# Local-attention layers on one core: finer pieces of scores and values' sums, weights one layer ahead, the norm on POOL, and a new order of issue

## The chip, the cores and the metric

The kernel runs on one core of one Trainium2 chip. The metric is device time in microseconds of one execution. Three runs of the kernel before gave 5607.32, 5605.51 and 5598.71 us; the median is 5605.51 us. One more execution was taken with the hardware profiler, and every duration below comes from it.

## The reference

The input is 16 sequences of 256 rows and 128 columns, float32. Four blocks follow one another, each as `x = x + layernorm(block(layernorm(x)))`. The first three (attention with low-rank weights, a routed expert layer, plain attention) are not touched by the change. The fourth is a stack of six layers, and it takes more than half of the time:

```
def attn_layer(x, Wqkv, qs, ksc, Wo):
    q, k, v = split(x @ Wqkv)            # 16 heads of 64
    q = l2norm(q) * qs;  k = l2norm(k) * ksc
    q = q*cos*scale + rotate_half(q)*sin*scale
    k = k*cos/scale + rotate_half(k)*sin/scale
    return local_attention(q, k, v) @ Wo # windows of 32: a row sees its own window and the one before
def ffn_layer(x, g, bln, W1, b1, W2, b2):
    a, gate = split(layernorm(x)*g + bln) @ W1 + b1
    return a * gelu(gate) @ W2 + b2
for i in range(6):
    x = attn_layer(shift_tokens(x), ...) + x
    x = ffn_layer(shift_tokens(x), ...) + x
```

`shift_tokens` takes the right half of the columns from the row before. `l2norm` divides each head's row by `maximum(norm, 1e-12)`.

## The kernel before

**One unit of work is one sequence in one layer.** There are 6 x 16 = 96 of them, numbered n; layer n // 16, sequence n % 16. Each unit is cut into some hundred named operations (`xT`, `pq0`, `sk1`, ...), each of which is a handful of instructions of one engine. The string `PERIOD` (line 770) lists all operation names once, each with a lag: at step s, `pq0:2` works on unit s - 2. `block4` (line 779) runs the steps one after another and, in each step, goes through the list from left to right. So several units are in flight, each in another part of its work.

**The list is the order of issue.** The class `InOrder` (line 35) ties each instruction of an engine to the one issued before it on the same engine, DMA issues on SyncE (SP) among them. An engine never takes a later instruction first: an operation that waits holds everything that stands behind it on its engine.

**What the names mean**, with t = 0 or 1 for the two halves of 128 rows, and a, b for halves of the heads:

- TensorE: `xT` transposes x; `pq`, `pk`, `pv` project (4 matmuls of 512 columns each); `tq`, `tk` transpose q and k; `sc` are the scores (128 small matmuls a half); `pe` transposes the exponentials; `pc` are the values' sums (128 small matmuls a half); `wo`, `gh`, `w2` are the output and feed-forward products; `gx` transposes the normed rows.
- VectorE: `a` multiplies the projection with the rotary tables; `r` sums the squares; `ms` and `mx` read the scores from PSUM, mask them and take their maximum; `sm` sums the exponentials; `y1` and `y0` add to x; `bn` takes mean and variance for the feed-forward norm; `xn` is that norm; `st` is the gate.
- ScalarE: `s` squares, `l` does Ln and Exp for the inverse norm, `x` is the exponential, `c..`, `ce`, `cc`, `cv` and `xc` copy PSUM to SBUF, `gg` is gelu (between two table loads).
- POOL: `h` and `m` finish the rotation and the scaling, `sb` subtracts the maximum, `n` normalises, `rs` raises the variance to the power -0.5.
- SP, all by DMA: `dv0` (16 DMAs) and `dv1` (14) spread v, one DMA for each window and half of the heads, into the windowed tile `vw`, each value once for its own window and once as the next window's past; `xs` (3 DMAs) moves x shifted by a row into the tile `xs` for `bn`; `W...` load weights.
- Units of layer 0 also pass `i1`, `i2`, `i3` (keep a copy, then norm), units of layer 5 `f1` to `f4` (norm, add, store).

**Buffers.** PSUM is two pools: `ps_p` with 3 buffers of 128x1024 (projections, `sc`, `pc`, two thirds of `gh`) and `ps_1` with 2 buffers of 128x512 (everything else). `xs`, `kT`, `vw` exist twice and are used by even and odd units.

**Weights** have one buffer each for `wo`, `w1`, `w2`, and five for the three parts of Wqkv. `Wqk` loads two parts and `Wv` the third, 512 KB each, at a layer's first unit; the v part needs the buffer of a q part that the layer before still uses.

Near the operations of the prediction the list of before reads, on each engine in its order:

```
SP:   dv0:3  dv1:3  xs:4  tb:0  Wqk:0
DVE:  ... ak1:3 bn:5 rk1:3 aq0:2 xn:5 rq0:2 ak0:2 ms0:3 ...  sm1:3 y1:4 aq1:2 rq1:2
ACT:  sk1:3 ce0b:4 xc:1 lq1:3 sq0:2 ck0a:3 ce1a:4 cv0:3 ...
POOL: hq1:3 mq1:3 rs:5 hk1:3 mk1:3 hq0:2 hk0:2 sb0:3 mq0:2 sb1:3 mk0:2 n0:3 n1:3
```

Of the kernel before, what the change touches and what calls it, by code (L numbers as in the profile page):

```python
# [1 line left out]

# [9 lines left out]
FP = mybir.dt.float32  # L12
# [52 lines left out]
class Net:  # L65
# [690 lines left out]
    def table(self, ins):  # L756
# [14 lines left out]
        xT:1 pq0:2 Wv:1 sk1:3 hq1:3 ce0b:4 pe1a:4 xc:1 lq1:3 ak1:3 mq1:3 sq0:2 tk0a:3 bn:5 i1:0 ck0a:3 pc0:4  # L771
        rk1:3 aq0:2 ce1a:4 rs:5 i2:0 tk0b:3 cv0:3 xn:5 i3:0 hk1:3 lk1:3 ck0b:3 pk0:2 cc0:4 tq1a:3 pe1b:4 dv0:3
        mk1:3 sk0:2 cq1a:3 rq0:2 sc0:3 ak0:2 tq1b:3 ms0:3 dv1:3 ce1b:4 tk1a:3 ck1a:3 pc1:4 hq0:2 cq1b:3 tk1b:3
        ck1b:3 mx0:3 hk0:2 sb0:3 w2:7 W2:6 y0:7 f1:7 cc1:4 gx:5 sc1:3 xg:5 lq0:2 rk0:2 mq0:2 x0:3 ms1:3 mx1:3
        f2:7 gh:5 W1:4 sb1:3 lk0:2 gg:5 pv1:2 pq1:2 sm0:3 f3:7 x1:3 wo:4 Wo:3 mk0:2 sq1:2 st:5 n0:3 sm1:3 f4:7
        cv1:2 y1:4 aq1:2 tq0a:2 pk1:2 n1:3 tq0b:2 rq1:2 cq0a:2 xs:4 cq0b:2 tb:0 pe0a:3 pv0:2 ce0a:3 pe0b:3 Wqk:0
# [14 lines left out]
    def layer_ops(self, ctx):  # L791
# [13 lines left out]
        rope = self.load(cp, "rope", ins["rope"].rearrange("k (t p) d -> p k t d", p=128), [128, 4, 2, LH])  # L805
# [5 lines left out]
        nc.gpsimd.memset(tiny[:, 1:2], EPS)  # L811
# [111 lines left out]
        def moments(n, src):
            st = self.small.tile([128, 2, 6], FP, name="bn_st")
            mv = put(n, "mv", self.small.tile([128, 2, 2], FP, name="bn_mv"))
            for t in range(2):
                nc.vector.bn_stats(st[:, t, :], src[:, t, :])
            for t in range(2):
                nc.vector.bn_aggr(mv[:, t, :], st[:, t : t + 1, :])
            ve = put(n, "ve", self.small.tile([128, 2], FP, name="bn_ve"))  # L930
            nc.vector.tensor_tensor(ve, mv[:, :, 1], tiny[:, 1:2].to_broadcast([128, 2]), ALU.add)

        def inverse(n):
            rstd = put(n, "rstd", self.small.tile([128, 2], FP, name="bn_rstd"))
            nc.gpsimd.tensor_tensor(rstd, take(n, "ve"), self.half.to_broadcast([128, 2]), ALU.pow)

        def norm(n, dst, src):
            mv, rstd = take(n, "mv"), take(n, "rstd")
            for t in range(2):
                nc.vector.scalar_tensor_tensor(  # L940
                    dst[:, t, :],
                    src[:, t, :],
                    mv[:, t, 0:1],
                    rstd[:, t : t + 1].to_broadcast([128, D]),
                    ALU.subtract,
                    ALU.mult,
                )
# [94 lines left out]
        @by("r", heads_of)  # L1042
        def _(n, k, t):
            r = put(n, ("r", k, t), pool.tile([128, NH], FP, name="r", bufs=6))
            sq = take(n, ("sq", k, t)).rearrange("p (h d) -> p h d", d=LH)
            nc.vector.tensor_reduce(r, sq, AX.X, ALU.add)
            nc.vector.tensor_tensor(r, r, tiny[:, 0:1].to_broadcast([128, NH]), ALU.max)

        @by("l", heads_of)
        def _(n, k, t):  # L1050
            r = get(n, ("r", k, t))
            nc.scalar.activation(r, r, AF.Ln)
# [38 lines left out]
        def _(n, t):  # L1091
            v = put(n, ("v", t), pool.tile([128, 2, 8, LH], FP, name="v"))
# [17 lines left out]
        @by("sc", tiles_of)  # L1110
        def _(n, t):
            s = put(n, ("s", t), ps_p.tile([128, 2, 8, 64], FP, name="sc", tag="p"))
            qT, kT = take(n, ("qT", t)), kTs[n % 2]
            for c in range(8):
# [66 lines left out]
        @by("pc", tiles_of)  # L1181
        def _(n, t):
            p = put(n, ("pc", t), ps_p.tile([128, 2, 4, 128], FP, name="pc", tag="p"))
            eT, vw = (take(n, ("eT", t, 0)), take(n, ("eT", t, 4))), vws[n % 2]
            for d in range(4):
                for q in range(4):
                    for odd in range(2):
                        c = 2 * d + odd
                        for j in range(2):
                            r, o = slice(64 * j, 64 * j + 64), 64 * (j ^ odd)  # L1190
                            nc.tensor.matmul(
                                p[o : o + 64, odd, d, 32 * q : 32 * q + 32],
                                lhsT=vw[r, 4 * t + q, c, :],
                                rhs=eT[c // 4][r, c % 4, 32 * q : 32 * q + 32],
                                start=True,
                                stop=True,
                            )
# [7 lines left out]
        def _(n):  # L1205
            po = put(n, "po", ps_1.tile([128, 2, D], FP, name="po", tag="w"))
            for t in range(2):
                cT = take(n, ("cT", t))
                for c in range(8):
                    nc.tensor.matmul(po[:, t, :], lhsT=cT[:, c, :], rhs=w["o"][:, c, :], start=c == 0, stop=c == 7)  # L1210
# [38 lines left out]
        def _(n):  # L1249
# [153 lines left out]
```

## Time and profile before

| | us |
|---|---|
| median of the three runs | 5605.51 |
| profiled execution, its own time | 5580.84 |
| its span, first to last instruction | 5579.1 |
| first three blocks, to the first transpose of the six layers | 2157.5 |
| six layers, from there to the end | 3421.6 |
| layers 1 to 4: from the first unit's `xT` of layer 1 (2661.8) to that of layer 5 (4901.3), 64 steps | 2239.5, or 35.0 a step |
| TensorE busy in 2638 to 3197, about layer 1 | 521.2 of 559.0 |
| VectorE, ScalarE, POOL busy there | 471.5, 358.5, 414.0 |

A busy time says how long an engine had an instruction in work, and nothing on whether the end waits for it. The granted clock of TensorE is 0.98 of full speed in that stretch. In the rows below, "idle before" is the time in which the engine had nothing in work just before such an instruction, and the name behind the arrow is what ended it; SPq is the DMA-issuing sequencer of SyncE. Nearly all lines of the fourth block are shown as L45, which is the helper in `InOrder`, so tiles' names tell the operations apart: `vw<-v` is `dv`, `xs<-x` is the shift, `bn_st` is `bn`, `x<-po` is `y0` or `y1`.

### The profile page before, as it was taken

How to read it: one execution, taken by the hardware profiler on the slowest of the kernel's cores; microseconds unless marked ns; L12 is line 12 of the kernel's file. 1: busy time of each engine (PE TensorE's matmuls, PEld its weight loads, DVE VectorE, ACT ScalarE, POOL GpSimd, SP SyncE). 2: the span in 40 equal slices, each digit the busy share in tenths (PEclk: the TensorE clock that was granted, in tenths of full speed). 3: DMA queues.
4: the chain of work that ended last, by engine and by line, in shares of the span. 5: the costliest groups of instructions: out<-in, count | busy, mean ns of one | idle time of the engine just before them, and what ended most of it. 6: DMA issues, size and time to landing. Idle time of an engine off the chain costs nothing.

```text
span 5579.1 us, 171669 instructions
## 1 busy us (share of the span) xinstructions
PE 4647.6 (83%) x74492; PEld 3449.9 (62%) x74492; DVE 4023.8 (72%) x6623; ACT 2761.0 (49%) x4751; POOL 2835.4 (51%) x2042
## 2 busy tenths in 40 slices
PE   7888754444489996999899989998999899999997
PEld 5555543333356664667677767776777667667776
DVE  3443228988743335889788878887888788878996
ACT  1222212333322224766566666666666666666664
POOL 1000012223210005777677767777777777767774
PEclk9999766767788888999999999999999999999998
DMA  1000000000000001322222222222222222222322
GB/s 28 1 1 1 1 0 11 1 0 1 1 3 1 1 1 44 73 65 68 71 71 64 64 71 68 66 65 73 68 69 60 75 66 66 64 72 70 73 68 59
DMA packets 222003, 240.87 MB, mean 43 GB/s; under 512 B 107747, under 2 KB 124598, under 8 KB 221110
## 3 DMA queue, kind: packets, MB, share of 16 engines
q1 hardware_dynamic: 221254, 229.90, 17.2%
q8 instruction: 590, 9.67, 0.8%
q14 instruction: 159, 1.30, 0.1%
HBM read 24.19 MB, written 4.19 MB: 5 GB/s over the span
## 4 chain that ended last, share of the span: by engine, by line
PE 66%; DVE 17%; issue 6%; ACT 4%; POOL 3%; SPq 2%; DMA 2%; ACTq 0%; POOLq 0%; DVEq 0%
PE pp L45 15%; PE po L45 7%; PE pc L45 7%; PE s L201 6%; PE pt L45 6%; PE sc L45 5%; PE ph L45 4%; PE pe L45 2%; PE s L213 2%; SPq L45 2%; DVE w L714 2%; PE pc L294 2%; DMA xs<-x 2%; DVE a L45 1%; DVE nm L257 1%
## 5 line engine op out<-in xcount | busy, mean ns | idle before, releaser
L45 POOL TENSOR_TENSOR a<-a 128x512 f32<-128x512 f32 x768 | 968.4, 1282 | 391.5 <-DVE a L45 390.2
L45 PE MATMUL pp<-part,xT 128*128 128x512 f32 x2304 | 1087.9, 602 | 3.0 <-DVE a L45 2.2
L45 DVE TENSOR_TENSOR a<-pp,tab 128x2048 f32<-128x2048 f32 x384 | 876.7, 2283 | 118.1 <-ACT sq L45 108.3
L45 POOL TENSOR_TENSOR am<-a,r 128x1024 f32<-128x1024 f32 x384 | 731.4, 1905 | 278.6 <-issue 244.9
L126 POOL TENSOR_TENSOR bn_rstd<-bn_ve,half 128x2 f32<-128x2 f32 x128 | 92.5, 724 | 1361.6 <-DVE bn_mv L122 1248.2
L45 PEld LDWEIGHTS pp<-part,xT 128*128 128x128 f32 x2304 | 415.8, 194 | 344.8 <-issue 319.2
L45 PE MATMUL pc<-eT,vw 64*64 64x32 f32 x24576 | 467.0, 222 | 91.3 <-issue 89.6
L45 PEld LDWEIGHTS pc<-eT,vw 64*64 64x64 f32 x24576 | 433.1, 136 | 137.0 <-issue 130.2
L45 PE MATMUL pt<-ident,am 128*128 128x128 f32 x3072 | 474.6, 283 | 23.2 <-POOL am L45 9.1
L45 DVE TENSOR_REDUCE r<-sq 128x16 f32<-128x1024 f32 x384 | 463.9, 1208 | 0.0
L45 PEld LDWEIGHTS pt<-ident,am 128*128 128x128 f32 x3072 | 357.0, 144 | 145.8 <-issue 109.4
L45 POOL TENSOR_TENSOR e<-e,mx 128x1024 f32<-128x1024 f32 x192 | 365.2, 1902 | 133.6 <-DVE mx L45 130.4
L45 ACT COPY kT<-pt 128x512 f32<-128x512 f32 x384 | 223.0, 581 | 417.5 <-PE pt L45 417.3
L45 ACT ACTIVATE sq<-pp 128x1024 f32<-128x1024 f32 x384 | 395.1, 1029 | 44.1 <-PE pp L45 43.9
L730 PE MATMUL pw<-ident,w 128*128 128x128 f32 x512 | 114.9, 416 | 353.7 <-ACT w L715 353.7
L45 PEld LDWEIGHTS po<-wo,cT 128*128 128x128 f32 x3072 | 358.1, 192 | 45.1 <-issue 44.5
L45 POOL TENSOR_TENSOR e<-e,sm 128x1024 f32<-128x1024 f32 x192 | 362.4, 1905 | 9.1 <-ACT sq L45 4.5
L45 ACT COPY qT<-pt 128x512 f32<-128x512 f32 x384 | 225.9, 590 | 272.1 <-PE pt L45 272.1
L45 PE MATMUL po<-wo,cT 128*128 128x128 f32 x3072 | 358.5, 275 | 0.0
L45 PE MATMUL sc<-kT,qT 64*32 64x64 f32 x24576 | 324.0, 230 | 38.3 <-issue 25.6
L257 DVE TENSOR_REDUCE nm<-s 128x2 f32<-128x512 f32 x256 | 159.1, 685 | 263.3 <-PE s L201 263.3
L45 PEld LDWEIGHTS sc<-kT,qT 64*32 64x32 f32 x24576 | 280.0, 107 | 87.8 <-issue 52.5
(221 smaller groups left out, 9167.4 us busy)
## 6 DMA issues: line engine op xcount, KB each, us to landing
vw<-v SPq DMA_DIRECT2D x2880, 64.0 KB
part<-in_L_ffn_Wqkv SPq DMA_DIRECT2D x18, 512.0 KB
xs<-x SPq DMA_DIRECT2D x96, 64.0 KB
xs<-x SPq DMA_DIRECT2D x96, 63.5 KB
wo<-in_Wo SPq DMA_DIRECT2D x6, 512.0 KB
x<-in_L_attn_hidden_states SPq DMA_DIRECT2D x8, 256.0 KB
kept<-x SPq DMA_DIRECT2D x16, 128.0 KB
xend<-kept SPq DMA_DIRECT2D x16, 128.0 KB
```

What stands on the lines that cost most here:

```text
L45: ins = trace(*args, **kw)
L126: nc.gpsimd.tensor_tensor(rstd, ve, self.half.to_broadcast([128, n]), ALU.pow)
L201: nc.tensor.matmul(s[:, i, o : o + 128], lhsT=lhs[r, g, lcols], rhs=rhs[r, g, rcols.start + o : rcols.start + o + 128], start=not masked, ...
L213: nc.tensor.matmul(s[:, :, diag], lhsT=self.ident_bf, rhs=mask[:, 0:n, :], start=True, stop=False)
L257: nc.vector.tensor_reduce(nm[:, 1, gs[0] : gs[1] + 1, 32 * j + NMROW], s, AX.X, ALU.max, negate=True)
L294: nc.tensor.matmul(pc[32 * j : 32 * j + 32, i, cols], lhsT=va[:, t, 4 * (g + i) + j, :], rhs=e[j][:, g + i, :], start=t == 0, stop=t == 1,)
L714: nc.vector.tensor_tensor(w, w, hh.unsqueeze(1).to_broadcast([128, RH, NE]), ALU.mult)
L730: nc.tensor.matmul(pw[:, c, :], lhsT=w[:, h, bass.ts(c, 128)], rhs=self.ident, is_transpose=True, start=h == 0, stop=h == RH - 1,)
```

## The change

The diff does six things.

1. `sc` and `pc` of each half become four operations each (`sc00` to `sc13`, `pc00` to `pc13`), 32 matmuls an operation; the number and the shape of the matmuls stay. The PSUM tile is allocated by the first of the four and released after the last.
2. Weights of the next layer are loaded in 18 pieces (12 of Wqkv, 4 of Wo, 2 of W1), one DMA a step and two in a layer's last four steps, by the new operation `W` at the end of the list. Wqkv has six buffers, Wo and W1 two. All of layer 0 is loaded at step 0. The rotary table is loaded from HBM into the table's tile for each layer and scaled there.
3. The norm (`xn`, `i3`, `f3`) goes from VectorE to POOL, and the addition of epsilon goes from VectorE (end of `bn`) to POOL (start of `rs`).
4. The maximum with 1e-24 at the end of `r` on VectorE becomes a Relu with bias -1e-24 and a bias of 1e-24 in Ln, on ScalarE.
5. `sq` and `v` share one set of three buffers (before, two each); `qT` has three (before, four).
6. `PERIOD` is written anew, with other lags and another order on every engine.

```diff
     PERIOD = """
-        xT:1 pq0:2 Wv:1 sk1:3 hq1:3 ce0b:4 pe1a:4 xc:1 lq1:3 ak1:3 mq1:3 sq0:2 tk0a:3 bn:5 i1:0 ck0a:3 pc0:4
-        rk1:3 aq0:2 ce1a:4 rs:5 i2:0 tk0b:3 cv0:3 xn:5 i3:0 hk1:3 lk1:3 ck0b:3 pk0:2 cc0:4 tq1a:3 pe1b:4 dv0:3
-        mk1:3 sk0:2 cq1a:3 rq0:2 sc0:3 ak0:2 tq1b:3 ms0:3 dv1:3 ce1b:4 tk1a:3 ck1a:3 pc1:4 hq0:2 cq1b:3 tk1b:3
-        ck1b:3 mx0:3 hk0:2 sb0:3 w2:7 W2:6 y0:7 f1:7 cc1:4 gx:5 sc1:3 xg:5 lq0:2 rk0:2 mq0:2 x0:3 ms1:3 mx1:3
-        f2:7 gh:5 W1:4 sb1:3 lk0:2 gg:5 pv1:2 pq1:2 sm0:3 f3:7 x1:3 wo:4 Wo:3 mk0:2 sq1:2 st:5 n0:3 sm1:3 f4:7
-        cv1:2 y1:4 aq1:2 tq0a:2 pk1:2 n1:3 tq0b:2 rq1:2 cq0a:2 xs:4 cq0b:2 tb:0 pe0a:3 pv0:2 ce0a:3 pe0b:3 Wqk:0
+        xT:1 pv1:3 cc1:5 lk1:3 x1:4 hq1:3 tk0a:3 pq0:2 mq1:3 xc:1 tk0b:3 dv0:3 f2:8 hk1:3 sm1:4 n1:4 ck0a:3
+        mk1:3 cv1:3 pk0:2 ck0b:3 sq0:2 f3:8 sc00:3 rq0:2 pe0a:4 sk0:2 sc01:3 tq1a:3 aq0:2 ce0a:4 dv1:3 f4:8
+        sc02:3 cq1a:3 wo:5 rk0:2 lq0:2 y1:5 tq1b:3 sc03:3 xs:5 ak0:2 tk1a:3 cq1b:3 bn:5 i1:0 ms0:3 pc00:4
+        ck1a:3 pe0b:4 hq0:2 mq0:2 pc01:4 tk1b:3 mx0:3 pq1:2 ce0b:4 rs:5 i2:0 tq0a:2 ck1b:3 pc02:4 sq1:2
+        tq0b:2 cq0a:2 cq0b:2 xn:5 i3:0 hk0:2 pc03:4 rq1:2 pv0:2 aq1:2 lk0:2 cc0:4 pe1a:4 sb0:3 sc10:3 ce1a:4
+        gx:5 xg:5 mk0:2 sc11:3 x0:3 pe1b:4 sc12:3 gh:5 ce1b:4 sm0:3 cv0:2 pc10:4 sc13:3 w2:7 W2:6 ms1:3 n0:3
+        pc11:4 mx1:3 pk1:2 gg:5 pc12:4 st:5 sb1:3 lq1:2 sk1:2 rk1:2 y0:7 f1:7 ak1:2 pc13:4 W:0
     """
...
+            def parts(k, j):
+                c = bass.ts(j, 256)
+                src = ins["L1_ffn_Wqkv"][i][:, k * inner : (k + 1) * inner]
+                load("qkv"[k], j, c, [inner], src[:, c], name="part", bufs=6)
...
+            for _ in range(2 if b >= B - 4 else 1):
+                if b > 0 and w["next"]:
+                    w["next"].pop(0)()
...
-            ve = put(n, "ve", self.small.tile([128, 2], FP, name="bn_ve"))
-            nc.vector.tensor_tensor(ve, mv[:, :, 1], tiny[:, 1:2].to_broadcast([128, 2]), ALU.add)
 
         def inverse(n):
             rstd = put(n, "rstd", self.small.tile([128, 2], FP, name="bn_rstd"))
-            nc.gpsimd.tensor_tensor(rstd, take(n, "ve"), self.half.to_broadcast([128, 2]), ALU.pow)
+            nc.gpsimd.tensor_scalar(rstd, get(n, "mv")[:, :, 1], EPS, None, ALU.add)
+            nc.gpsimd.tensor_tensor(rstd, rstd, self.half.to_broadcast([128, 2]), ALU.pow)
 
         def norm(n, dst, src):
...
-                nc.vector.scalar_tensor_tensor(
...
+                nc.gpsimd.tensor_scalar(
+                    dst[:, t, :], src[:, t, :], mv[:, t, 0:1], rstd[:, t : t + 1], ALU.subtract, ALU.mult
                 )
...
-            nc.vector.tensor_tensor(r, r, tiny[:, 0:1].to_broadcast([128, NH]), ALU.max)
...
-            nc.scalar.activation(r, r, AF.Ln)
+            nc.scalar.activation(r, r, AF.Relu, bias=tiny[:, 1:2])
+            nc.scalar.activation(r, r, AF.Ln, bias=tiny[:, 0:1])
...
-            v = put(n, ("v", t), pool.tile([128, 2, 8, LH], FP, name="v"))
+            v = put(n, ("v", t), pool.tile([128, 2, 8, LH], FP, name="v", tag="sv", bufs=3))
...
-        @by("sc", tiles_of)
-        def _(n, t):
-            s = put(n, ("s", t), ps_p.tile([128, 2, 8, 64], FP, name="sc", tag="p"))
-            qT, kT = take(n, ("qT", t)), kTs[n % 2]
-            for c in range(8):
+        fourths = {f"{t}{d}": (t, d) for t in range(2) for d in range(4)}
+
+        @by("sc", fourths)
+        def _(n, t, d):
+            if d == 0:
+                put(n, ("s", t), ps_p.tile([128, 2, 8, 64], FP, name="sc", tag="p"))
...
+            for c in (2 * d, 2 * d + 1):
...
+        @by("pc", fourths)
+        def _(n, t, d):
+            if d == 0:
+                put(n, ("pc", t), ps_p.tile([128, 2, 4, 128], FP, name="pc", tag="p"))
```

Read engine by engine, the new list gives these orders around `bn`:

```
SP:   dv0:3  dv1:3  (f4:8)  xs:5  (i1:0)  W2:6  (f1:7)  W:0
DVE:  sm1:4 rq0:2 aq0:2 rk0:2 y1:5 ak0:2 bn:5 (i1:0) ms0:3 mx0:3 rq1:2 aq1:2 sm0:3 ms1:3 mx1:3 st:5 rk1:2 y0:7 ak1:2
ACT:  cc1:5 lk1:3 x1:4 xc:1 ck0a:3 cv1:3 ck0b:3 sq0:2 sk0:2 ce0a:4 ... cc0:4 ce1a:4 xg:5 x0:3 ce1b:4 cv0:2 gg:5 lq1:2 sk1:2
POOL: hq1:3 mq1:3 hk1:3 n1:4 mk1:3 hq0:2 mq0:2 rs:5 (i2:0) xn:5 (i3:0) hk0:2 sb0:3 mk0:2 n0:3 sb1:3
PE:   ... wo:5 tq1b sc03 tk1a pc00 pe0b pc01 tk1b pq1:2 tq0a pc02 tq0b pc03 pv0:2 pe1a sc10 gx:5 sc11 pe1b sc12 gh:5 ...
```

## The prediction

> **What bounds the kernel now.** I read the page, then the timeline of some steps in the middle, then the chain of waits at the start of a layer, and last single rows. The page first:
>
> ```profile
> span 5579.1 us, 171669 instructions
> ...
> PE 4647.6 (83%) x74492; PEld 3449.9 (62%) x74492; DVE 4023.8 (72%) x6623; ACT 2761.0 (49%) x4751; POOL 2835.4 (51%) x2042
> ...
> PE 66%; DVE 17%; issue 6%; ACT 4%; POOL 3%; SPq 2%; DMA 2%; ACTq 0%; POOLq 0%; DVEq 0%
> ```
>
> TensorE carries the chain. A step (one `xT` to the next) is 35.0 us in the mean of layers 1 to 4; the best steps are 32.1. From the chain's pieces of one step TensorE needs about 31.2: projections 24 x 0.43 = 10.3, transposes of q, k and the exponentials 48 x 0.109 = 5.2, `wo` 3.6, `w2` 1.3, `gh` 2.8, `gx` and `xT` 0.45, scores 3.1, values' sums 4.4. What stands above is idle PE within `pc` (57.0 us in the 57 steps from 3000 to 5000 us, put down to issue), a lower granted clock in single steps, and two slow steps at each layer's start.
>
> The timeline shows how full SP is, though SPq is 2% of the chain (start, length, engine, operation, count):
>
> ```profile
> 4005.65 22.57 SPq L45 DMA_DIRECT2D vw<-v  x30
> ...
> 4028.26 0.42 DVE L45 TENSOR_TENSOR x<-po,x 128x256 f32<-128x256 f32 x1 [1.23 <-PE po L45]
> ...
> 4028.72 4.13 SPq L45 DMA_DIRECT2D xs<-x  x3
> ...
> 4033.25 0.38 PE L45 MATMUL xTp<-ident,x 128*128 128x128 f32 x2
> ...
> 4035.15 0.48 DVE L45 BATCH_NORM_STATS2 bn_st<-xs 128x6 f32<-128x128 f32 x2
> ...
> 4038.32 22.96 SPq L45 DMA_DIRECT2D vw<-v  x30
> ```
>
> Issuing `dv0` and `dv1` takes SP 22.57 us of a 32 us step, `xs` 4.13 more, and 6.2 us pass from the end of `y1` (4028.68) to the first VectorE instruction that can read `xs` (6.2 is also the least of all steps where VectorE waits for it). Over the 96 bursts of 30 issues the median is 22.2 us, from 18.9 to 23.8. Before, this is free: `xs` is ready to go just when the burst ends, and nothing between `bn` and the next `dv0` links the two.
>
> At a layer's start the link exists, and the chain shows its price (start, length, what):
>
> ```profile
> 2683.86 3.45 PE pp L45 x8
> 2687.32 0.33 SPq L45
> ...
> 2706.07 0.59 SPq L45
> 2706.75 0.67 SPq L45
> 2707.47 5.40 DMA xs<-x
> 2712.97 0.48 DVE bn_st L45 x2
> ```
>
> SP stood 24.6 us at the v weights' load, which waits for a buffer; the burst and `xs` queued behind it, and `bn` came 25.7 us after SP was let go. VectorE is in order, so everything after `bn` waited too; the two steps there take 42.4 and 38.4 us in the mean (about 13 us of loss a layer).
>
> **The change, part by part.**
>
> *Scores and sums in fourths.* Same matmuls; what can go is the idle PE inside them, about 1 us a step, as long as PE sets the end. It costs a longer hold of a PSUM buffer, counted below.
>
> *Weights.* The 24.6 us stall goes. One 128 KB piece a step is one more issue of 0.35 to 0.6 us (rows of the present weight loads), after `xs`, where SP would stand idle until `cv0`: nothing. Layer 0's 18 issues (about 9 us) run beside the memsets on POOL: +5. `W2` stays ahead of `dv0` and waits for `w2` of the same step: by PE's order 11.2 us after `bn`, 1.7 after `cv0`; with its issue 2.3 x 6 = +14.
>
> *VectorE relieved.* A step loses 4 maxima x 0.58, the addition 1.19 and two norms x 1.27: 6.0 us off an engine that was busy 29 of 35. It gains nothing unless VectorE is on the chain. ScalarE gets four Relus of about 0.2 to 0.3 on 22.3 us: hidden.
>
> *Norm on POOL.* No row has this operation on POOL. The nearest:
>
> ```profile
> L45 POOL TENSOR_TENSOR tab<-rope,scq 128x64 f32<-128x64 f32 x24 | 7.2, 324 | 0.0
> L724 POOL TENSOR_TENSOR w<-w,last 128x1 f32<-128x1 f32 x32 | 7.6, 238 | 297.4 <-ACT u L720 263.8 <-DVE pk L602 12.1 <-DVE sc L601 10.8
> L45 POOL TENSOR_TENSOR xend<-xend,x 128x256 f32<-128x256 f32 x16 | 11.6, 724 | 14.8 <-DMA xend<-kept 9.2 <-DVE x L45 5.3
> ...
> L45 DVE SCALAR_TENSOR_TENSOR xn<-xs,bn_mv,bn_rstd x192: 334/1346/2055, 2256.8 to 5560.4; 128x128 f32<-128x128 f32 x192
> ```
>
> Between 64 and 256 columns the line gives 0.45 for 128, so 0.90 for two; the low end is a memset of 128x128 (0.20 each), the high end VectorE's 1.3 each. The addition: 0.20, between a memset's 0.10 and the 0.24 above; the power is 0.70. Against this move speaks the Trainium skill, "GPSIMD Engine Reference", Engine selection: elementwise work belongs on VectorE, POOL being some 2 times slower for two inputs and about even for one. By the page two norms would be 0.7 on either engine; by the row VectorE needs 2.7, stretched from 0.33 each. So the sum below is 38.0 by the rows and 37.8 by the page: the engine is not what hurts, the place is.
>
> *The new order.* On SP, `xs:5` stands behind `dv1`; `bn` comes two VectorE operations after `y1`. On POOL, `rs` and `xn` stand ahead of `hk0` and `sb0`. On ScalarE, `x0` (which needs `sb0`) stands ahead of `cv0`, and the next step's `dv0` needs `cv0`. So there is a closed loop, once round per step:
>
> - `bn` 0.70 (4035.15 to 4035.85)
> - `rs` 0.90, `xn` 0.90 (estimates above), `hk0` 2.50, `sb0` 1.90 on POOL
> - `x0` 0.97, `ce1b` 0.48, `cv0` 1.04 on ScalarE (start to next start, the last one in full)
> - two hand-overs 0.10
> - 30 issues of `dv` 22.2
> - end of burst to `bn` 6.3 (4061.27 to 4067.57, a step where SP was late)
>
> Sum **38.0 us**, and no engine can shorten it, since each takes its list in order. PE's 31.2 then has 6.8 us of slack. I look for it in front of `pv0`: `ps_p` has three buffers, `pv0` needs the one of `sc0`, read by `ms0`, which stands behind `bn`. PE goes on 2.0 us after `bn`; from `pv0` on 12.4 us to the step's end and 11.9 to the end of `wo` make `y1` ready 26.9 us after `bn`, while the burst ends at 31.7: 4.8 us of cover, so late PE work (gaps, lower clock) mostly hides. The Trainium skill's rule for this place ("DMA: Bandwidth & Descriptors", Rules for kernel authors) is to issue a DMA early, compute, and wait for it late; here the wait follows after one operation of 2.3 us. By the rule alone, with SP free at `y1`, PE would stand 0.4 + 6.2 + 0.7 + 1.2 = 8.5 less the 6.9 us of PE work between `wo` and `pv0`: 1.6 us, a step of 32.8. By the rows the issue itself is what is late.
>
> **The sum.** Layers 1 to 4: 64 x 38.0 - 2239.5 = +193. Layer 0: `i2` and `i3` join the loop (+1.8); twelve full steps took 413.8 (2248.1 to 2661.8) and will take 11 x 39.8 + 38.0 = 475.8: +62. Layer 5: the store of `f4` stands on SP ahead of `xs`, and POOL reaches `f4` some 2.5 us after the burst (estimate from POOL's order); 15 steps took 528.0, will take 15 x 38.0 + 8 x 2.5 = 590: +62. One lag more at the end, like one of the seven present steps of the drain (150 us): +20. With +5 and +14: **+356**. On the profiled execution's 5580.8 that is 5937, on the median of 5605.5, which I forecast, **5960**.
>
> **The rivals.**
>
> - *Loop, dearer (16%).* Norms at 1.3 us each make it 39.7: about 6135. If `dv0` waited for the whole of `vw`, that is for `pc13`, the loop would be 14.4 + 22.2 + 6.3 = 42.9: about 6405. Against it: the second, fourth and later DMAs of a burst now wait for TensorE one by one, so regions are told apart.
> - *Loop, cheaper (13%).* The bursts after SP had stood still took 18.9. Then 34.7 a step: about 5660, with 20.0 about 5760.
> - *PE still binds (faster, 8%).* If a turn of the loop stays below PE, steps go to 32.5 (its best now, without gaps): layers 1 to 4 -160, layers 0 and 5 -37, end +25, about 5435. For it: 13 us a layer and the gaps are really lost now. It decides below 32.5 us for the loop, a burst under 16.7 or 0.56 an issue; the fastest burst has 0.63.
> - *No change (3%).* A loop of about 34.5 by chance cancels what the layer starts give.
>
> The forecast itself has 60%, with a loop of 37.0 to 39.5, so 5870 to 6100. Some 0.2% is what a measurement can tell from no change. Faster 0.08, same 0.03, slower 0.89. The range takes the cheaper bursts down to 20 and the dearer norms with some waits: 5740 to 6240.
>
> **What would show it.** Steps of 38 us; VectorE waiting 4 us or more for `xs` before `bn` in every step; PE idle before `pp`, ended by `e` of VectorE; bursts of `vw` still 22 us; the chain mostly SPq, with POOL, ScalarE and DMA; no 24.6 us wait on SP; gaps in `pc` gone or hidden. I am wrong if steps are near 33, if `bn` does not wait, or if bursts are below 19 us.

## The result and the profile after the change

The changed kernel takes 6090.65 us in the median of four runs (6083.42 to 6099.34), beside 5604.05 us for the kernel before. The ratio is 1.087, with an interval of 1.0851 to 1.0889: 487 us slower. The prediction was 5960, with a range of 5740 to 6240: the side and the range held, the size of the loss was put some 130 us too low.

The two profiled spans (5579.1 and 6089.8 us) differ by 510.7 us. Cut at the first transpose (`xT`) of each layer, as the prediction cut them:

| part | before, us | after, us | difference | predicted |
|---|---|---|---|---|
| first three blocks, and layer 0's loads | 2157.5 | 2163.4 | +5.9 | +5 |
| layer 0 | 504.3 | 596.4 | +92.1 | +62 |
| layers 1 to 4 | 2239.5 | 2540.9 | +301.4 | +193, and 9 for `W2` |
| layer 5, to its last `xT` | 528.0 | 604.5 | +76.5 | +62 |
| end | 149.8 | 184.6 | +34.8 | +20 |

A step of layers 1 to 4 is 39.70 us; before it was 34.99, and 38.0 were predicted (38.1 with `W2`).

From the page of the changed kernel: span, busy engines, the chain that ended last, and two rows (busy, mean ns of one, idle before and its releaser). Its lines are L46 where they were L45.

```profile
span 6089.8 us, 172394 instructions
...
PE 4988.9 (82%) x74492; PEld 3454.1 (57%) x74492; DVE 3438.3 (56%) x5855; ACT 2939.7 (48%) x5135; POOL 3054.4 (50%) x2426
...
PE 20%; DMA 5%; POOL 3%; DVE 2%; SPq 2%; ACT 1%; issue 1%; POOLq 0%; DVEq 0%; ACTq 0%
...
L46 PE MATMUL pp<-part,xT 128*128 128x512 f32 x2304 | 1260.2, 675 | 312.6 <-DVE e L46 297.0
...
L46 DVE BATCH_NORM_STATS2 bn_st<-xs 128x6 f32<-128x128 f32 x192 | 47.8, 286 | 666.8 <-DMA xs<-x 666.7
```

The same two rows of the kernel before:

```profile
L45 PE MATMUL pp<-part,xT 128*128 128x512 f32 x2304 | 1087.9, 602 | 3.0 <-DVE a L45 2.2
...
L45 DVE BATCH_NORM_STATS2 bn_st<-xs 128x6 f32<-128x128 f32 x192 | 46.0, 282 | 65.4 <-DMA xs<-x 65.1
```

VectorE is relieved by 586 us of busy time, and the kernel is slower all the same. VectorE now stands 666.7 us at `xs` (65.1 before), and TensorE 297.0 us at `e` of VectorE, which is `ms0` behind `bn`; before, TensorE stood 3.0 us in all ahead of these rows. The chain names only some 34% of the span; it can't be used to tell which loop sets the end, so that is read from one step. The timeline of the changed kernel (start, length, engine, operation, count, idle before):

```profile
4012.29 0.49 DVE L46 BATCH_NORM_STATS2 bn_st<-xs 128x6 f32<-128x128 f32 x2 [5.50 <-DMA xs<-x]
...
4013.09 0.23 POOL L46 TENSOR_SCALAR bn_rstd<-bn_mv 128x2 f32<-128x2 f32 x1 [6.45 <-DVE bn_mv L46]
4013.40 0.72 POOL L46 TENSOR_TENSOR bn_rstd<-bn_rstd,half 128x2 f32<-128x2 f32 x1
4014.22 1.58 POOL L46 TENSOR_SCALAR xn<-xs,bn_mv,bn_rstd 128x128 f32<-128x128 f32 x2
4015.77 2.49 POOL L46 TENSOR_TENSOR a<-a 128x512 f32<-128x512 f32 x2
4018.22 1.91 POOL L46 TENSOR_TENSOR e<-e,mx 128x1024 f32<-128x1024 f32 x1
...
4020.16 1.06 ACT L46 ACTIVATE e<-e 128x1024 f32<-128x1024 f32 x1 [0.77 <-POOL e L46]
...
4021.59 1.02 ACT L46 COPY v<-pp 128x1024 f32<-128x1024 f32 x1
4022.63 22.02 SPq L46 DMA_DIRECT2D vw<-v  x30
4033.58 1.02 ACT L46 COPY v<-pp 128x1024 f32<-128x1024 f32 x1
4041.85 0.43 DVE L46 TENSOR_TENSOR x<-po,x 128x256 f32<-128x256 f32 x1 [1.25 <-PE po L46]
4044.76 4.25 SPq L46 DMA_DIRECT2D xs<-x  x3
4051.01 0.49 DVE L46 BATCH_NORM_STATS2 bn_st<-xs 128x6 f32<-128x128 f32 x2 [6.54 <-DMA xs<-x]
...
4052.88 3.78 PE L46 MATMUL pp<-part,xT 128*128 128x512 f32 x4 [3.20 <-DVE e L46]
```

Down to the second `bn`, and without the second copy of `v` (`cv1`) and `x<-po` (`y1`), these lines are the predicted loop once round, from `bn` to `bn` in 38.72 us: POOL, ScalarE's `x0` and `cv0`, the burst of 30 issues, `xs`, `bn`. But two other paths come in as late or almost.

One is `cv1`. It ends at 4034.60, just when the last 14 issues (`dv1`, 10.0 us of the burst) begin. SP's own list of waits in 3000 to 5000 us (total, times, longest) has

```profile
SPq L46 <- ACT v L46: 536.6, 47, 12.7
...
SPq L46 <- ACT kT L46: 66.0, 46, 2.7
```

The first line is the wait of `dv0` for `cv0`. The second stands ahead of `dv1`; the list names the copy of `kT` next to `cv1`, but in 57 of the 64 steps of layers 1 to 4 `dv1` starts within 0.1 us of the end of `cv1`. SP stands still there for 0.99 us in the mean, against 0.06 in the kernel before. So the way from `cv0` over the rest of ScalarE's list to `cv1` is some 0.9 us longer than the first 16 issues: the loop that sets the step goes from `bn` to `cv0` as predicted, on to `cv1` (22.9 us after `bn` in the mean), and over `dv1` alone to `xs`. The predicted loop has 0.9 us of slack beside it.

The other is `y1`, which ends at 4042.28, only 2.5 us before `xs` can be issued. It closes a third loop, through TensorE.

This third loop is so near because TensorE's wait has a second price. Windows of 2 us in the same kernel, PE alone (busy, granted clock, share of DMA, GB/s):

```profile
4051.00:4053.00 2.00, 0.12 (x1) 0.56 0.00 1
4053.00:4055.00 2.00, 2.00 (x3) 0.50 0.01 4
4055.00:4057.00 2.00, 2.00 (x5) 0.50 0.00 0
4057.00:4059.00 2.00, 2.00 (x71) 0.73 0.03 8
4059.00:4061.00 2.00, 2.00 (x42) 1.00 0.00 0
```

After 3.20 us of standing at `pv0` (the last line of the timeline), TensorE works at half its clock for some 5 us. `pv0` takes 3.78 us there, and 1.98 where TensorE did not wait, and the two small operations behind it lose 0.6 more.

### The profile page after: what moved, and what is told of

Read it like the earlier page. It is cut to its first block, busy times and chain, and to the rows that moved or that the text cites. A ratio compares the mean times of both kernels' runs of the same rounds, so it can differ in the third digit from the quotient of the medians.

```text
span 6089.8 us, 172394 instructions
## 1 busy us (share of the span) xinstructions
PE 4988.9 (82%) x74492; PEld 3454.1 (57%) x74492; DVE 3438.3 (56%) x5855; ACT 2939.7 (48%) x5135; POOL 3054.4 (50%) x2426
## 5 line engine op out<-in xcount | busy, mean ns | idle before, releaser
L46 PE MATMUL pp<-part,xT 128*128 128x512 f32 x2304 | 1260.2, 675 | 312.6 <-DVE e L46 297.0
L46 POOL TENSOR_TENSOR a<-a 128x512 f32<-128x512 f32 x768 | 959.2, 1271 | 26.6 <-DVE a L46 18.9
L46 DVE TENSOR_TENSOR a<-pp,tab 128x2048 f32<-128x2048 f32 x384 | 875.9, 2281 | 0.0
L46 PEld LDWEIGHTS pp<-part,xT 128*128 128x128 f32 x2304 | 435.8, 210 | 656.2 <-issue 327.5
L46 POOL TENSOR_TENSOR am<-a,r 128x1024 f32<-128x1024 f32 x384 | 731.5, 1905 | 48.6 <-PE pt L46 33.9
L46 DVE TENSOR_REDUCE r<-sq 128x16 f32<-128x1024 f32 x384 | 466.4, 1215 | 318.1 <-ACT sq L46 318.1
L46 PEld LDWEIGHTS pc<-eT,vw 64*64 64x64 f32 x24576 | 460.2, 134 | 199.8 <-issue 158.4
L46 PE MATMUL pc<-eT,vw 64*64 64x32 f32 x24576 | 535.2, 222 | 14.7 <-ACT v L46 14.3
L46 ACT COPY eT<-pe 128x512 f32<-128x512 f32 x384 | 226.0, 589 | 622.2 <-PE pe L46 622.1
L46 ACT ACTIVATE sq<-pp 128x1024 f32<-128x1024 f32 x384 | 389.4, 1038 | 264.4 <-PE pp L46 186.2
L46 PE MATMUL pt<-ident,am 128*128 128x128 f32 x3072 | 484.5, 281 | 22.4 <-ACT xT L46 14.0
L46 POOL TENSOR_TENSOR e<-e,mx 128x1024 f32<-128x1024 f32 x192 | 365.4, 1903 | 243.9 <-DVE mx L46 228.0
L46 PEld LDWEIGHTS pt<-ident,am 128*128 128x128 f32 x3072 | 350.6, 141 | 201.3 <-issue 88.4
L46 DVE BATCH_NORM_STATS2 bn_st<-xs 128x6 f32<-128x128 f32 x192 | 47.8, 286 | 666.8 <-DMA xs<-x 666.7
L46 POOL TENSOR_TENSOR e<-e,sm 128x1024 f32<-128x1024 f32 x192 | 365.8, 1905 | 101.6 <-DVE sm L46 99.6
L46 POOL TENSOR_SCALAR bn_rstd<-bn_mv 128x2 f32<-128x2 f32 x128 | 29.1, 227 | 742.6 <-DVE bn_mv L46 742.5
L46 DVE TENSOR_REDUCE sm<-e 128x16 f32<-128x1024 f32 x192 | 233.3, 1215 | 283.4 <-ACT e L46 283.4
L46 ACT COPY qT<-pt 128x512 f32<-128x512 f32 x384 | 224.7, 585 | 334.8 <-PE pt L46 323.1
L46 PE MATMUL po<-wo,cT 128*128 128x128 f32 x3072 | 368.4, 278 | 8.7 <-ACT eT L46 8.7
L46 PE MATMUL sc<-kT,qT 64*32 64x64 f32 x24576 | 362.2, 229 | 10.2 <-DVE e L46 7.1
```

What stands on the lines that cost most here:

```text
L46: ins = trace(*args, **kw)
```

## The experiments

All are timed against the kernel before on the same chip (5583 to 5589 us). "Step" is the mean of layers 1 to 4, and so are the pieces of a step where nothing else is said.

### Cutting single links of the loop

**`cv0` next to `pv0`.** No link from `bn` through POOL and `x0` to `dv0` is left; `cv1`, and with it `dv1`, still stands behind `x0` in ScalarE's list.

```diff
-        tq0b:2 cq0a:2 cq0b:2 xn:5 i3:0 hk0:2 pc03:4 rq1:2 pv0:2 aq1:2 lk0:2 cc0:4 pe1a:4 sb0:3 sc10:3 ce1a:4
-        gx:5 xg:5 mk0:2 sc11:3 x0:3 pe1b:4 sc12:3 gh:5 ce1b:4 sm0:3 cv0:2 pc10:4 sc13:3 w2:7 W2:6 ms1:3 n0:3
+        tq0b:2 cq0a:2 cq0b:2 xn:5 i3:0 hk0:2 pc03:4 rq1:2 pv0:2 cv0:2 aq1:2 lk0:2 cc0:4 pe1a:4 sb0:3 sc10:3 ce1a:4
+        gx:5 xg:5 mk0:2 sc11:3 x0:3 pe1b:4 sc12:3 gh:5 ce1b:4 sm0:3 pc10:4 sc13:3 w2:7 W2:6 ms1:3 n0:3
```

> cv0 is moved in the list from behind ce1b to right behind pv0, so it no longer stands behind x0. Loop theory (SP's burst of vw between cv0 and bn): the loop through x0 and cv0 shrinks by about 5 us a step, but a second loop lies right behind it, through cv1: in the changed kernel cv1 ends 22.3 us after bn (4012.29 to 4034.60), and 14 issues of about 10.3 and 6.35 from burst to bn make 39.0 again. gg starts about 1 us earlier, so steps of 38 to 39 and 6000 to 6090 us. Rival 1 (the path through POOL's norm, x0 and cv0 is the only loop): steps near 33.7, 5550 to 5620 us. Rival 2 (the longer hold of PSUM by the fourths of sc and pc sets the step): no change, 6090 us.

Measured: 6194.25 us, ratio 1.1094 (1.1064 to 1.1124); step 40.99. From `bn` to the burst it is now 6.6 us in the median instead of 10.4, but the burst lasts 27.5 instead of 22.4. Within it SP stands still twice: 2.5 us ahead of the fourteenth issue, put down to `pc`, and 3.4 us ahead of `dv1`, for `cv1`. ScalarE's waits in 3000 to 5000 us (total, times, longest) say why `cv1` is late:

```profile
ACT v L46 <- PE pp L46: 343.7, 49, 13.2
```

ScalarE is in order too. It stands 7 us a step at `cv0`, since `pv0` itself comes behind `bn` (through `ms0` and the PSUM buffer of `sc0`), and `cv1` and all else on ScalarE comes later by it: `cv1` ends 24.2 us after `bn` instead of 22.9, and the step is 1.3 us longer too. So cutting the predicted loop at `cv0` gains nothing, because the loop through `cv1` sets the step before and after the cut.

**`cv1` next to `pv1` as well.**

```diff
-        xT:1 pv1:3 cc1:5 lk1:3 x1:4 hq1:3 tk0a:3 pq0:2 mq1:3 xc:1 tk0b:3 dv0:3 f2:8 hk1:3 sm1:4 n1:4 ck0a:3
-        mk1:3 cv1:3 pk0:2 ck0b:3 sq0:2 f3:8 sc00:3 rq0:2 pe0a:4 sk0:2 sc01:3 tq1a:3 aq0:2 ce0a:4 dv1:3 f4:8
+        xT:1 pv1:3 cv1:3 cc1:5 lk1:3 x1:4 hq1:3 tk0a:3 pq0:2 mq1:3 xc:1 tk0b:3 dv0:3 f2:8 hk1:3 sm1:4 n1:4 ck0a:3
+        mk1:3 pk0:2 ck0b:3 sq0:2 f3:8 sc00:3 rq0:2 pe0a:4 sk0:2 sc01:3 tq1a:3 aq0:2 ce0a:4 dv1:3 f4:8
```

> cv0 right behind pv0 as before, and cv1 right behind pv1 at the head of ScalarE's step. Loop theory: cv0 ends about 5 us after bn, dv0 needs 12, cv1 is done by then, so bn to bn is 5 + 22.3 + 0.1 + 6.3 = 33.7, with y1 nearly as late by TensorE's order: steps of 33.6 to 35, 5560 to 5690 us. Rival 2 (PSUM held longer by the fourths): no change, 6090 us.

Measured: 6200.5 us, ratio 1.11 (1.1072 to 1.1129); step 41.27. Missed as well. Now SP waits for `y1`, 2.7 us a step: neither loop through `cv` sets the end any more, the one through TensorE does, and waits that ScalarE and VectorE hand on have made it longer:

```profile
PE sc L46 <- DVE a L46: 98.0, 48, 2.2
PE pt L46 <- ACT xT L46: 63.8, 49, 1.3
PE pp L46 <- DVE e L46: 50.6, 48, 6.2
```

**The norm back on VectorE** (the addition stays on POOL).

```diff
-                nc.gpsimd.tensor_scalar(
-                    dst[:, t, :], src[:, t, :], mv[:, t, 0:1], rstd[:, t : t + 1], ALU.subtract, ALU.mult
+                nc.vector.scalar_tensor_tensor(
+                    dst[:, t, :],
+                    src[:, t, :],
+                    mv[:, t, 0:1],
+                    rstd[:, t : t + 1].to_broadcast([128, D]),
+                    ALU.subtract,
+                    ALU.mult,
```

> The norm alone goes back to VectorE, its place in the list unchanged. Loop theory: the two norms of 0.79 us leave POOL's stretch between bn and x0, 1.6 us a step (3.2 in layer 0): steps of about 38, 5900 to 5970 us, although VectorE gets slower. If the norm on POOL were the whole loss: 5600. If it plays no part, as when PSUM or the weights set the step: 6090 us or slower.

Measured: 6267.94 us, ratio 1.1223 (1.1194 to 1.1252). From `bn` to the burst it takes only 0.7 us less in the median, and the burst is 24.4 us, with 2.9 us of waiting for `cv1` ahead of `dv1`: `cv1` ends 24.8 us after `bn` instead of 22.9, about what the step loses (41.44 instead of 39.70). Why ScalarE comes to `cv1` later was not followed. In this order the norm is better off on POOL; the engine of the norm is not the fault.

**`dv1` behind `xs`.** SP issues only `dv0` ahead of `xs`.

```diff
-        mk1:3 cv1:3 pk0:2 ck0b:3 sq0:2 f3:8 sc00:3 rq0:2 pe0a:4 sk0:2 sc01:3 tq1a:3 aq0:2 ce0a:4 dv1:3 f4:8
-        sc02:3 cq1a:3 wo:5 rk0:2 lq0:2 y1:5 tq1b:3 sc03:3 xs:5 ak0:2 tk1a:3 cq1b:3 bn:5 i1:0 ms0:3 pc00:4
+        mk1:3 cv1:3 pk0:2 ck0b:3 sq0:2 f3:8 sc00:3 rq0:2 pe0a:4 sk0:2 sc01:3 tq1a:3 aq0:2 ce0a:4 f4:8
+        sc02:3 cq1a:3 wo:5 rk0:2 lq0:2 y1:5 tq1b:3 sc03:3 xs:5 dv1:3 ak0:2 tk1a:3 cq1b:3 bn:5 i1:0 ms0:3 pc00:4
```

> One name moves: dv1 goes behind xs in the list, so that SP issues xs after dv0. Loop theory: bn no longer waits for the last 14 issues. The next limits are TensorE's path from pv0 to y1 plus 6.2 us (33), and sq1, which shares buffers with v and may wait for dv1 to land (35.5): steps of 33 to 36, 5480 to 5790 us. Rival 2 (PSUM held by the fourths) and a theory that the number of SP's issues itself is the bound: no change, 6090 us.

Measured: 5919.86 us, ratio 1.0587 (1.0554 to 1.062): 171 us better than the changed kernel, so the burst ahead of `xs` was a gate, as predicted. But 336 us of the loss stay. The step is 37.10 (36.4 in the median), against 39.70 and, before, 34.99; and layer 0 takes 664 us instead of 596: `dv1` now stands between `xs` and the copy to `kept` on SP, and POOL waits some 6 us a step for that copy. The waits of VectorE and of PE:

```profile
DVE bn_st L46 <- DMA xs<-x: 221.6, 56, 4.2
```

```profile
PE pc L46 <- ACT v L46: 55.3, 54, 1.0
PE pp L46 <- DVE e L46: 40.7, 54, 1.1
```

VectorE still stands 4 us at `xs` in each step. The loop that is left goes `pv0`, TensorE's work up to `wo`, `y1`, issue and flight of `xs`, `bn`, `ms0`, `pv0`, with 0.8 us of waiting ahead of `pv0` and 1.0 ahead of `pc10`. None of the times that the theory of one loop gave for these runs had held, and they had one fault in common: each cut or shortened a link that not all loops have, while the loops share another. All go through `y1`, `xs` and `bn` within one step.

### Cutting the link that all loops share

**One lag more for `bn` and what belongs to it.** Same order, same instructions; `bn` in step s works on the unit whose `xs` was issued in step s - 1.

```diff
-        sc02:3 cq1a:3 wo:5 rk0:2 lq0:2 y1:5 tq1b:3 sc03:3 xs:5 ak0:2 tk1a:3 cq1b:3 bn:5 i1:0 ms0:3 pc00:4
+        sc02:3 cq1a:3 wo:5 rk0:2 lq0:2 y1:5 tq1b:3 sc03:3 xs:5 ak0:2 tk1a:3 cq1b:3 bn:6 i1:0 ms0:3 pc00:4
...
-        gx:5 xg:5 mk0:2 sc11:3 x0:3 pe1b:4 sc12:3 gh:5 ce1b:4 sm0:3 cv0:2 pc10:4 sc13:3 w2:7 W2:6 ms1:3 n0:3
+        gx:6 xg:6 mk0:2 sc11:3 x0:3 pe1b:4 sc12:3 gh:6 ce1b:4 sm0:3 cv0:2 pc10:4 sc13:3 w2:7 W2:6 ms1:3 n0:3
```

(`rs`, `xn`, `gg` and `st` go from 5 to 6 likewise.)

> The changed kernel with `bn` and all that belongs to its group (`rs`, `xn`, `gx`, `xg`, `gh`, `gg`, `st`) one step of lag later; order and instructions the same. Theory of three loops: all of them close because `bn` reads the `xs` that was issued after `y1` in the same step. With a lag between, none closes, `bn` never waits for its DMA, and TensorE sets the step again: 32.5 to 33.5 us in the middle layers, 5400 to 5560 us in all. Rival, the fourths' longer hold of PSUM (or POOL's longer chain to `sb0`) binds by itself: the step stays at 36 to 37 us as with `dv1` moved, 5880 to 5960. If neither is right and only the burst counts, no change: 6090.

Measured: 5576.24 us, ratio 0.9987 (0.9977 to 0.9998): 514 us better than the changed kernel. PE's list of waits in 3000 to 5000 us has one line, where the changed kernel waited 147.6 us for `e` alone; the second fence is the stretch of layers 1 to 4 (busy of PE, PEld, DVE, ACT, POOL, then the granted clock).

```profile
PE po L46 <- ACT eT L46: 2.6, 3, 0.9
```

```profile
2735.00:4909.40 2174.40, 2170.77 (x41221) 1526.24 (x41217) 1519.03 (x1600) 1549.45 (x2689) 1765.85 (x1313) 1.00 0.30 70
```

TensorE is busy in 2170.8 of 2174.4 us at full clock (0.93 in the changed kernel, 0.98 before), and nearly every step has 33.9 us. The loops are shown: with the one dependency moved, they are gone, and with them the half clock. Neither the hold of PSUM nor POOL's chain to `sb0`, the rival, keeps the step at 36 to 37 us. The total is 16 us above the expectation: the step is some 0.5 us above the 33.5 allowed, and layer 0 kept steps of about 40.5 us.

**The pieces of `sc` and `pc` together again**, in the list with the lag of 6: `sc00` to `sc03` stand where `sc03` stood, and so for the other three groups (the lines are wrapped here as in the list with lag 6).

```diff
-        mk1:3 cv1:3 pk0:2 ck0b:3 sq0:2 f3:8 sc00:3 rq0:2 pe0a:4 sk0:2 sc01:3 tq1a:3 aq0:2 ce0a:4 dv1:3 f4:8
-        sc02:3 cq1a:3 wo:5 rk0:2 lq0:2 y1:5 tq1b:3 sc03:3 xs:5 ak0:2 tk1a:3 cq1b:3 bn:6 i1:0 ms0:3 pc00:4
+        mk1:3 cv1:3 pk0:2 ck0b:3 sq0:2 f3:8 rq0:2 pe0a:4 sk0:2 tq1a:3 aq0:2 ce0a:4 dv1:3 f4:8
+        cq1a:3 wo:5 rk0:2 lq0:2 y1:5 tq1b:3 sc00:3 sc01:3 sc02:3 sc03:3 xs:5 ak0:2 tk1a:3 cq1b:3 bn:6 i1:0 ms0:3
...
```

> As the run with the lag of 6, but the four pieces of each `sc` and `pc` stand next to each other in the list, where the last one stood. If TensorE sets the step there, this shows what the spacing is worth by itself: idle TensorE inside the groups of small matmuls of about 1 us a step comes back, +64 to +100 us against the run with lag 6. Rival, the longer hold of a PSUM buffer by the spread pieces costs more than the gaps: this one is faster by 1 to 2 us a step, -100 to -190. If it is the same to 20 us, TensorE does not set the step.

Measured: 5625.05 us, ratio 1.0071 (1.0053 to 1.0089): 49 us slower than with the pieces apart; step 34.86 against 33.98. PE's waits here are

```profile
PE po L46 <- ACT eT L46: 45.5, 57, 2.0
PE pc L46 <- issue: 27.2, 17, 2.4
PE pe L46 <- ACT eT L46: 26.3, 58, 0.5
PE pt L46 <- ACT kT L46: 13.9, 58, 0.2
```

so the gaps within the small matmuls come back with 0.5 us a step, and TensorE waits 1.5 for ScalarE: 2.0 us of waits in all. Against that stands TensorE's busy time in layers 1 to 4, 32.8 us a step instead of 33.9. The net 0.9 us a step makes 77 us in layers 1 to 5; layer 0 is 27 us shorter. Pieces apart in program order are worth something, with the gaps half of what the prediction allowed and the rest from what ScalarE gets done meanwhile. That they cost more by their longer hold of PSUM is refuted.

**`i1` ahead of `xs`**, with the lag of 6, for layer 0.

```diff
-        sc02:3 cq1a:3 wo:5 rk0:2 lq0:2 y1:5 tq1b:3 sc03:3 xs:5 ak0:2 tk1a:3 cq1b:3 bn:6 i1:0 ms0:3 pc00:4
+        sc02:3 cq1a:3 wo:5 i1:0 rk0:2 lq0:2 y1:5 tq1b:3 sc03:3 xs:5 ak0:2 tk1a:3 cq1b:3 bn:6 ms0:3 pc00:4
```

> As the run with lag 6, and `i1` (the copy of x to `kept` and its mean and variance) moved from behind `bn` to behind `wo`, so that SP issues the copy ahead of `xs`. In the run with lag 6 layer 0 keeps steps of 40.5 us; theory: `i3` waits for the copy (3.8 us), `sb0`, `x0` and `cv0` stand behind it, and TensorE waits for `cv0`. Then layer 0 falls to 34 to 36 us a step: 5500 to 5540 us in all. Rival, the second mean and variance on VectorE and the second power and norm on POOL make layer 0's loop by themselves: 5560 to 5580.

Measured: 5529.79 us, ratio 0.9893 (0.9875 to 0.991), as expected. Layer 0 goes from 572.7 to 524.9 us, and its later steps are 34.5. It had been the same kind of loop: `y1`, `xs`, the copy to `kept` behind it on SP, `i3` on POOL waiting for that copy, `sb0`, `x0`, `cv0`, TensorE, `y1`.

**v in 10 DMAs instead of 30**, in the order of the changed kernel: v goes once to a tile in DRAM and from there four windows at a time into `vw`.

```diff
-            for q in range(4):
-                i = 4 * t + q
-                for j in range(2):
-                    src = v[32 * q : 32 * q + 32, j]
-                    nc.sync.dma_start(out=vw[64 * j + WIN : 64 * j + 2 * WIN, i], in_=src)
-                    if i < 7:
-                        nc.sync.dma_start(out=vw[64 * j : 64 * j + WIN, i + 1], in_=src)
+            vd = dram.tile([128, 2, inner // 2], FP, name="vd", bufs=4)
+            nc.sync.dma_start(out=vd, in_=v.rearrange("p j c d -> p j (c d)"))
+            for j in range(2):
+                src = vd[:, j].rearrange("(q p) x -> p q x", p=WIN)
+                to = vw.rearrange("p i c d -> p i (c d)")
+                last = 4 - t
+                nc.sync.dma_start(out=to[64 * j + WIN : 64 * j + 2 * WIN, 4 * t : 4 * t + 4], in_=src)
+                nc.sync.dma_start(out=to[64 * j : 64 * j + WIN, 4 * t + 1 : 4 * t + 1 + last], in_=src[:, :last])
```

> The changed kernel with v spread in 10 DMAs a step instead of 30 (v goes to a DRAM tile once, from there 4 windows at a time); same order. Theory: what SP spends on issuing is the gate, the burst falls from 22 to 6 to 9 us, the loops through `cv0` and `cv1` open, and the loop through TensorE is left: steps of 36 to 37 us as with `dv1` behind `xs`, 5880 to 5960 us. Rival, it is the moving of the bytes that takes the time, not the issue: SP waits, or `pc` waits for `vw` for longer, and the time is 6050 or more.

Measured: 6030.54 us, ratio 1.0801 (1.0783 to 1.0819); step 39.80, between the two expectations. SP issues `xs` right behind `y1`, so the issue is no longer the gate, and TensorE's list has no wait of `pc` for the DMAs of `vw`, as the rival would have it. But the loop through TensorE is longer than with `dv1` moved:

```profile
4030.32 4.54 PE L46 MATMUL ph<-xg,w 128*128 128x256 f32 x12 [3.07 <-ACT v L46]
```

`gh` waits 3.07 us for `cv0` and then takes 4.54 us, against 2.86 at full clock. Neither the changed kernel nor the one with `dv1` moved has this wait. It ends with `cv0`, which frees the PSUM buffer of `pv0`; why `gh` needs that buffer here and not there was not tried.

### Parts alone, in the order of before

**All weights in pieces**, with what the change does to make room: `sq` and `v` share three buffers, three of `qT`, the rotary table loaded per layer. Of the edit, the shared buffers:

```diff
-            sq = put(n, ("sq", k, t), pool.tile([128, inner], FP, name="sq"))
+            sq = put(n, ("sq", k, t), pool.tile([128, inner], FP, name="sq", tag="sv", bufs=3))
...
-            v = put(n, ("v", t), pool.tile([128, 2, 8, LH], FP, name="v"))
+            v = put(n, ("v", t), pool.tile([128, 2, 8, LH], FP, name="v", tag="sv", bufs=3))
```

> The kernel before with the weights alone changed (pieces one layer ahead, their buffers, the shared buffers of `sq` and `v`, three of `qT`, the rotary table by layer); the old list. Theory: the stop of 24.6 us on SP at each layer's start goes and with it about 13 us a layer: 5500 to 5545 us beside 5584 for the kernel before on this chip. Rival, the loss at the layer's start is taken elsewhere (the next wait is as late): 5570 to 5590. Second rival, one more issue a step or the fewer buffers cost something in every step: 5600 or more.

Measured: 5892.39 us, ratio 1.0538 (1.0509 to 1.0567); step 38.08. The stop on SP is gone, but ScalarE has a new wait:

```profile
ACT sq L46 <- DVE r L46: 206.2, 53, 4.0
```

`sq` waits for one of the three buffers in every step, 3.9 us. In the order of the changed kernel the same sharing costs little (31.7 us in the same 2000, for `vw<-v`). So this run told of the buffers, not of the stop.

**Wqkv alone in pieces.** Buffers of `sq` and `v`, Wo, W1, W2 and the table as before; three of `qT`.

```diff
-        @op("Wqk", when=first)
-        def _(n):
-            part(n, 0)
-            part(n, 1)
+                if j == 0:
+                    w["qkv"[k], i] = wp.tile([128, inner], FP, name="part", bufs=6)
+                src = ins["L1_ffn_Wqkv"][i][:, k * inner : (k + 1) * inner]
+                nc.sync.dma_start(out=w["qkv"[k], i][:, c], in_=src[:, c])
...
+            if i + 1 < DEPTH and b == 0:
+                w["next"] = pieces(i + 1)
+            if i + 1 < DEPTH and 0 < b <= 12:
+                w["next"].pop(0)()
```

> The kernel before with Wqkv alone in 12 pieces one layer ahead (six buffers; three of `qT` instead of four to make room; Wo, W1, W2, the rotary table and the buffers of `sq` and `v` as they were). Theory: what cost 308 us in the run with all weights in pieces was `sq` waiting for one of three buffers shared with `v`, and the stop of 24.6 us on SP is worth 13 us a layer: 5500 to 5545 us. Rival, the pieces themselves or the third `qT` buffer cost in every step: 5600 or more. Rival, the layer's start is lost anyway to the loads of Wo and W1: 5570 to 5590.

Measured: 5520.97 us, ratio 0.987 (0.985 to 0.989). The stop is worth 68 us, 13 to 14 a layer, as the profile of before had said. This is the lowest median of the study, 9 us below the new order with the lag of 6 and `i1` moved, and it keeps the old order.

**The same with VectorE relieved**: norm on POOL, Relu and Ln on ScalarE.

```diff
-            nc.vector.tensor_tensor(r, r, tiny[:, 0:1].to_broadcast([128, NH]), ALU.max)
...
-            nc.scalar.activation(r, r, AF.Ln)
+            nc.scalar.activation(r, r, AF.Relu, bias=tiny[:, 1:2])
+            nc.scalar.activation(r, r, AF.Ln, bias=tiny[:, 0:1])
...
-                nc.vector.scalar_tensor_tensor(
...
+                nc.gpsimd.tensor_scalar(
+                    dst[:, t, :], src[:, t, :], mv[:, t, 0:1], rstd[:, t : t + 1], ALU.subtract, ALU.mult
```

> As the run with Wqkv alone in pieces, and with the norm on POOL and the Relu and Ln on ScalarE (VectorE loses 6 us a step). Prediction's step: it gains nothing as long as VectorE is not on the chain: within 15 us of that run. Rival, VectorE's fill (29 of 35 us) delays `y1`, `ms` and `mx` and so TensorE now and then: 30 to 120 us faster. Second rival, POOL's longer list delays `sb0` and costs 20 to 60 us.

Measured: 5585.22 us, ratio 0.9993 (0.9979 to 1.0007), so 64 us slower than without. The relief gains nothing, as expected, but it does not stay within 15 us: the second rival is the nearest, POOL's longer list. Layer 0, where a second power and norm stand in that list, loses 41 us (510.0 to 551.1), layers 1 to 5 lose 23. TensorE has a new wait for POOL, of its transposes for `m`, 0.9 us a step:

```profile
PE pt L46 <- POOL am L46: 50.1, 48, 1.6
```

## Why the prediction was right, and where its sizes were off

**The mechanism held.** The step is set by a loop that closes because `bn` waits for an `xs` issued in the same step, behind a burst on SP; in the mean of layers 1 to 4 from `bn` to the burst it is 10.9 us, the burst 22.3, and on to `bn` 6.4. VectorE waits 6.8 us for `xs`, TensorE 3.1 for `ms0`, the 24.6 us stop is gone and so are the gaps in `pc`. One of the signs failed: the chain is not "mostly SPq" (2%).

**It was not one loop.** Three loops lie within a few us, and the one that the prediction drew is the second: between `cv0` and the last 14 issues ScalarE's list to `cv1` takes 0.9 us longer than the 16 issues that the sum counted there. So cutting the predicted loop by itself gained nothing. The third was hidden by the cover of `y1`, put at 4.8 us and measured at 2.5. TensorE's slack of 6.8 us was wrong as well: this list takes 33.9 us of TensorE with no wait in it, not the 31.2 summed from before, and the wait halves the clock. The Trainium skill ("TensorE: Matmul & The Clock Gate", HAM oscillation) has that rule: idle gaps of more than some 3.4 us cost the clock. The sum had left it out; in this trace gaps of 1.5 to 2.5 us mostly cost it already.

**The step of 38.0, mis-sized by 1.6:**

- *Two norms on POOL:* 0.90 estimated, 1.58 measured: 0.7 of the 1.6. Interpolating between rows of other operations by the number of columns was the weak step; the 0.7 that the prediction worked out from the skill's page was further off. The rival of the dearer loop, with norms at 1.3 each, named 39.7 us, the measured step; that is luck, since the norms took 0.79.
- *`W2`:* 2.3 expected, 6.7 measured (17.0 from `bn` to the burst instead of 10.3), 0.3 a step in the mean. SP's timeline there:

```profile
3628.52 0.40 SPq L46 DMA_DIRECT2D w<-in_W  x1
3628.96 0.49 SPq L46 DMA_DIRECT2D part<-in_L_ffn_Wqkv  x1
3629.49 0.43 SPq L46 DMA_DIRECT2D tab<-in_rope  x1
3629.97 0.58 SPq L46 DMA_DIRECT2D scq<-in_L_ffn_q_scale  x1
3630.59 0.43 SPq L46 DMA_DIRECT2D sck<-in_L_ffn_k_scale  x1
3631.13 21.22 SPq L46 DMA_DIRECT2D vw<-v  x30
```

  `bn` was at 3614.12, so `w2` is done 14.4 us after it instead of 11.2 (2.5 of that is half clock again: the same stretch from `pv0` takes 12.5 us here and 10.0 with the lag of 6), and then the piece and the table's three loads of that same step go ahead of the burst, 2.1 us that the sum had not placed there.
- *Hand-overs, `rs` and steps with a later `cv0`:* 0.3. *Burst to `bn`:* 6.4 instead of 6.3.
- *The burst itself:* 22.3 instead of 22.2. That this agrees is luck: 0.9 of it is the wait for `cv1`, and the issues alone take 21.4.

**Layer 0** lost 92 instead of 62: `i2` and `i3` take 2.5 us of POOL's time in a step rather than 1.8 (the norm again), on top of the longer loop. **Layer 5:** the eight steps with `f4` are 1.0 us longer than the same steps of layers 1 to 4, not 2.5; the longer step makes up for it. **The drain** took 35 instead of 20. The stop at the layer's start came out as said, and the relief of VectorE gained nothing, as said; that the norm on POOL costs something in the old order too was not foreseen. The fourths gave 0.9 us a step where they were tried, only half of it from the gaps.

What the change brought by itself can now be put beside that: 68 us for the stop and 49 for the pieces apart, against 514 that the loops cost. The lag of 6 gives those back and still ends only 7 us below the kernel before: it gains 65 us in layers 1 to 4 and 16 in layer 5, and loses 68 in layer 0 and some 10 at both ends. With `i1` moved as well it ends 59 us below. More is not to be had from waits in layers 1 to 4, since TensorE's work in this list is 33.9 us a step, against 32.1 in the best steps of before.

## What to carry to other kernels

In a hand-made order, follow each value that goes through a DMA to its reader: if the reader stands in the same turn of the loop, every queue on the way is part of a cycle; here one more turn of lag opened three of them at once and took no buffer. When cutting a link gains nothing, look for the link that all late paths share before cutting a second one. A wait that looks hidden on TensorE may not be free: here one of 2 us or more mostly bought the next few us at half clock. And before a burst is counted as one piece, look whether one of its later issues waits for something else.

## What the runs showed of the hardware

- Half clock came after shorter idle times than expected. In the changed kernel TensorE stood 3 us or more at `pv0` in 61 of 96 steps, and the four matmuls behind took 3.78 us in the median; after 2.5 to 3 us (22 steps) 3.46, with three at 1.98; after 1.5 to 2.5 us (11 steps) 3.0 to 3.8 in nine of them; after 0.5 to 1 us (2 steps) 1.97. With `dv1` behind `xs`, 12 steps of 1.0 to 1.5 us have a median of 1.98, with two at 3.31 and 3.68.
- Taking the groups of 128 small matmuls apart removes idle time within them (57.0 us in 57 steps before, none with the lag of 6) but has a price: with the lag of 6, TensorE's busy time is 33.9 us a step with them apart and 32.8 with them together. Part of it shows in the transposes: four of them take 0.53 to 0.60 us from start to start ahead of a group of small matmuls, and 0.44 between two projections.
- On POOL, `tensor_scalar` with two per-row operands on 128x128 float32 takes 0.79 us, and the addition on 128x2 0.23.
